# Rows of 450 words padded to 464, and the second cross attention in chunks of 512, 512, 512 and 66

## The chip, the core and the metric

The kernel runs on one core of a Trainium2 chip. The metric is the device time of one execution in microseconds (us). Before the change it is 2689.3 us, the median of three runs (2683.21 to 2691.54).

## What is computed

Two layers of a perceiver on 8 batches: 64 query tokens each, and a context of 1601 tokens, both 512 wide, in float32. Cut to what the change touches:

```python
x = x + xattn0(layernorm(x), ctx)   # 32 heads of 128, 8 key/value heads
x = x + mamba(layernorm(x))         # state-space scan over 64 steps
x = x + ternary_ffn(layernorm(x))
# second cross attention: one head, no weights
a = einsum('bqd,bkd->bqk', layernorm(x), ctx)
x = x + einsum('bqk,bkd->bqd', softmax(a), ctx)
x = x + self_attention(layernorm(x))
x = x + octonion_ffn(layernorm(x))
```

In the first cross attention, `k = ctx @ Wk + bk` and `v = ctx @ Wv + bv` are computed for all 1601 tokens, then `softmax(q k / sqrt(128)) v`. In the second, the scores are one 64 x 1601 table for each batch.

## The kernel before, in words

**The first cross attention** is most of the time (`x_all`). Its units are the 64 pairs of a batch and a key/value head. The context of a batch, transposed, stands in SBUF in four blocks of 384, 384, 384 and 450 tokens (`BLK`). `x_ctx` (line 295) brings each block in as four chunks of 128 channels: it loads a chunk into a staging tile `cst`, ScalarE copies it rounded (the "high" part, line 105), and GpSimd writes what is left over (the "low" part, line 106). The tile of a block is [128, 2, 4, width]: partition, high or low, chunk, token. The first three blocks lie in three buffers of the tile `cxb`, with rows of 384 words; the last block lies in the one buffer of `cxt`, with rows of 450 words. `cst` has rows of 450 words for all blocks. A product of two such operands is three matmuls: high by high, high by low, low by high.

- `x_v` (matmul at line 334) computes values for 128 tokens and two heads at a time: the block's tokens are the weights, `wv` with 256 columns is the moving operand. 12 matmuls for each token tile.
- `x_k` (line 363) computes a head's keys for one block: `wk` is the weights, the block with its 384 or 450 columns is the moving operand. 12 matmuls, then ScalarE and VectorE write the key tile `kt` (lines 108 and 109). `kt` is [128, 2, 450] whatever the block, three buffers.
- `x_s` (line 385) computes scores: a 128-token part of `kt` is the weights, `q` with 256 columns is moving. Three matmuls for each tile of tokens. Lines 388 and 392 take them out of PSUM and keep the maximum.
- `x_max`, `x_spread`, `x_exp`, `x_av`, `x_o` do the softmax and the product with the values for the unit before, between these steps. `x_wo` (line 511) is the output projection.

**The other layers** (`chain`) run for a group of two batches at a time, four groups. The first three run beside the first cross attention of later batches: `advance` lets a side chain go on as far as its planned cost (the numbers that the generators yield) says. Its work for VectorE, ScalarE and GpSimd is kept in program order (`Late`, `Side`); the rest of the order is set when the program is built, from a simulated time line (`schedule_with_timeline_sim=True`). The last group runs after the first cross attention, with other buffer counts (`tail`).

**The second cross attention** (`xattn1`, line 997) is one block of that chain. `scores` goes through the 1601 keys in parts of PSUM size: each entry of `GW` names the chunk of the score table and the widths of the loads. Each load brings `ctxT` columns for 4 chunks of 128 channels; four multiplications put two half sums into the upper and lower 64 partitions of PSUM (line 1021). ScalarE copies the lower half (line 1032), VectorE adds it to the upper half and writes a chunk of the table (line 1034). When all parts are there, VectorE takes a maximum by chunk (line 1040) and over the chunks (line 1041), and ScalarE computes the exponential by chunk with its sum (line 1044). `values` transposes the table in tiles of 128 keys (line 1059) and multiplies with `ctxN` (line 1077). Where a side chain runs, the same instructions are recorded at line 65, the helper that keeps them in order.

Before, the table has three chunks of 512, 512 and 577 (`SW`), the last one filled by two parts of 384 and 194 columns. In a side chain each chunk is a buffer of the tag `b2`, which has five buffers, each as large as the largest tile of the tag: the 578 words of the third chunk. In the last group the table is one tile `bc` of 1602 words.

Of the kernel before, what the change touches and what calls it, by code (L numbers as in the profile page):

```python
# [9 lines left out]
FR = mybir.dt.float32r  # L10
AF = mybir.ActivationFunctionType
ALU = mybir.AluOpType
AX = mybir.AxisListType
# [3 lines left out]
P = 128  # L17
D = 512
NC = 4
T = 64  # L20
# [4 lines left out]
NT = 13  # L25
TAIL = LK - 12 * P
BLK = [(0, 384), (384, 384), (768, 384), (1152, 450)]
LB = 3
DIN = 1024
NCH = 8  # L30
# [20 lines left out]
def rows_of(t):  # L51
    return TAIL if t == 12 else P
# [26 lines left out]
class Kernel:  # L79
# [133 lines left out]
    def q_ln(self, p):  # L213
# [9 lines left out]
        for g in range(ng):  # L223
            n = min(P, NQ - g * P)
            xs = self.sb("S", [P, 2, 256], pool=self.xp, bufs=SB)
            xt.append(xs[:n].rearrange("p a b -> p (a b)"))
# [68 lines left out]
    def x_ctx(self, b, k):  # L295

        nc = self.nc
        o, w = BLK[k]
        if k == LB:
            t = self.sb("cxt", [P, 2, NC, BLK[LB][1]], FR, pool=self.xp, bufs=1)  # L300
        else:
            t = self.sb("cxb", [P, 2, NC, BLK[0][1]], FR, pool=self.xp, bufs=3)
        for c in range(NC):
            st = self.sb("cst", [P, BLK[LB][1]], pool=self.xp, bufs=3)
            nc.sync.dma_start(out=st[:, :w], in_=self.i["ctxT"][b, c, :, o : o + w])
            self.split(t[:, 0, c, :], t[:, 1, c, :], st[:, :w], eng=nc.gpsimd)
        self.ctxb[(b, k)] = t
# [6 lines left out]
    def at(self, t):  # L314

        blk = min(t // 3, LB)
        return blk, (t - 3 * blk) * P
# [36 lines left out]
    def x_k(self, b, i, blk, w):  # L354

        nc = self.nc
        wd = BLK[blk][1]
        cx = self.cblk(b, blk)
        ps = self.px.tile([P, D], FP, name=self.nm("k_ps"), tag="kv", bufs=KVB)
        k = 0  # L360
        for c in range(NC):
            for a, m in ((0, 0), (0, 1), (1, 0)):
                nc.tensor.matmul(ps[:, :wd], lhsT=w[:, a, c, :], rhs=cx[:, m, c, :], start=k == 0, stop=k == 11)  # L363
                k += 1
        kt = self.sb("kt", [P, 2, BLK[LB][1]], FR, pool=self.xp, bufs=3)
        self.split(kt[:, 0, :wd], kt[:, 1, :wd], ps[:, :wd], bias=self.bk[:, i : i + 1])
        return kt

    def x_s(self, b, i, st):

        nc = self.nc
        q = self.q[(b, i)]
        S = self.S.setdefault((b, i), [])
        if st == 0:
            self.mf[(b, i)] = self.sb("mx", [P, 2, 256], pool=self.xp, bufs=1)
        mx = self.mf[(b, i)]
        for g in [(2 * st, 2 * st + 1)] + ([(12,)] if st == 5 else []):
            sp = self.px.tile([P, 2, 256], FP, name=self.nm("s_ps"), tag="kv", bufs=KVB)
            r = P
            for gi, t in enumerate(g):  # L380
# [3 lines left out]
                for k, (a, m) in enumerate(((0, 0), (0, 1), (1, 0))):  # L384
                    nc.tensor.matmul(sp[:r, gi, :], lhsT=kt[:, a, o : o + r], rhs=q[:, m, :], start=k == 0, stop=k == 2)  # L385
            s = self.sb("S", [P, 2, 256], pool=self.xp, bufs=SB)
            n = len(g)
            nc.scalar.copy(s[:r, :n], sp[:r, :n])  # L388
            if n == 1:
                nc.vector.tensor_tensor(mx[:r, 0], sp[:r, 0], mx[:r, 0], ALU.max)  # L390
            elif len(S) > 0:
                nc.vector.tensor_tensor(mx, sp, S[0] if len(S) == 1 else mx, ALU.max)  # L392
            S.append(s)
        if st == 5:
# [602 lines left out]
    def xattn1(self, bs, x, xo):  # L997

        nc, i = self.nc, self.i
        lt = self.lnT(x, P, hl=False)  # L1000
        GW = [(0, (256, 256)), (1, (256, 256)), (2, (192, 192)), (2, (194,))]
        SW = [512, 512, 577]
        TS = ((0, 4), (4, 8), (8, NT))

        def scores(k, b):
            q0 = k * T
            if self.tail:
                s = self.sb("bc", [T, LP])
                S = [s[:, :512], s[:, 512:1024], s[:, 1024:]]
            else:  # L1010
                S = [self.sb("b2", [T, 512]), self.sb("b2", [T, 512]), self.sb("b2", [T, 578])]
            o = 0
            for m, ws in GW:
                ps = self.acc()
                e = 0
                for w in ws:
                    cx = self.sb(self.tc4, [P, NC, 256])
                    nc.sync.dma_start(out=cx[:, :, :w], in_=i["ctxT"][b, :, :, o + e : o + e + w].rearrange("c p k -> p c k"))
                    for c in range(2):
                        for half in range(2):  # L1020
                            nc.tensor.matmul(  # L1021
                                ps[half * T : half * T + T, e : e + w],
                                lhsT=lt(2 * half + c, 0)[:, q0 : q0 + T],
                                rhs=cx[:, 2 * half + c, :w],
                                start=c == 0,
                                stop=c == 1,
                            )
                    e += w
                    if self.tail:
                        yield 2  # L1030
                lo = self.sb("b2", [T, D])
                nc.scalar.copy(lo[:, :e], ps[T:, :e])
                so = o - 512 * m
                nc.vector.tensor_tensor(S[m][:, so : so + e], ps[:T, :e], lo[:, :e], ALU.add)
                o += e
                if not self.tail:
                    yield 2 * len(ws)
            nm = self.sb("s1m", [T, 4])
            for m in range(3):
                nc.vector.tensor_reduce(nm[:, m : m + 1], S[m][:, : SW[m]], AX.X, ALU.max)  # L1040
            nc.vector.tensor_reduce(nm[:, 3:4], nm[:, 0:3], AX.X, ALU.max, negate=True)
            sm2 = self.sb("s1s", [T, 4])
            for m in range(3):
                nc.scalar.activation(S[m][:, : SW[m]], S[m][:, : SW[m]], AF.Exp, bias=nm[:, 3:4], accum_out=sm2[:, m : m + 1])
            sm = sm2[:, 3:4]
            nc.vector.tensor_reduce(sm, sm2[:, 0:3], AX.X, ALU.add)
            nc.vector.reciprocal(sm, sm)
            yield 3
            return S, sm

        def values(k, b, S, sm):
            q0 = k * T
            pts = []
            for m, (t0, t1) in enumerate(TS):
                pt = self.sb("b2", [P, 5, T])
                tp = self.acc().rearrange("p (t q) -> p t q", q=T)
                for t in range(t0, t1):
                    r = rows_of(t)
                    nc.tensor.transpose(tp[:r, t - t0, :], S[m][:, (t - t0) * P : (t - t0) * P + r], self.ident[:T, :T])
                e = min(t1, 12) - t0  # L1060
                nc.scalar.copy(pt[:, :e, :], tp[:, :e, :])
                if t1 == NT:
                    nc.scalar.copy(pt[:TAIL, e, :], tp[:TAIL, e, :])
                pts.append(pt)
                yield 2
            ps = self.acc()
            for t in range(0, NT, 2):
                two = t + 1 < NT
                r = rows_of(t)
                cx = self.sb(self.tc4, [P, 2, D])  # L1070
                if two:
                    nc.sync.dma_start(out=cx, in_=i["ctxN"][b, t * P : (t + 2) * P, :].rearrange("(u p) d -> p u d", p=P))
                else:
                    nc.sync.dma_start(out=cx[:r, 0], in_=i["ctxN"][b, t * P : t * P + r, :])
                m = min(t // 4, 2)
                for u in range(1 + two):
                    nc.tensor.matmul(  # L1077
                        ps[u * T : u * T + T], lhsT=pts[m][:r, t + u - TS[m][0], :], rhs=cx[:r, u], start=t == 0, stop=t + u >= NT - 2
                    )
                if self.tail:  # L1080
                    yield 1 + two
            if not self.tail:
# [407 lines left out]
```

## Time and profile before

| | |
|---|---|
| median of three runs | 2689.3 us |
| the profiled execution | 2687.19 us, of it the span of the profile 2685.1 us |
| mean granted TensorE clock | 0.983 |
| value projection, line 334 | 4992 matmuls, 1536 of them on `cxt` |
| key projection, line 363 | 3072 matmuls, 768 of them on `cxt` |
| scores, line 385 | 2496 matmuls, the weights from `kt` |
| second cross attention's scores, line 1021 | 448 matmuls in the trace (each multiplication is two) |
| loads of the last block, `cst` | 32 of 225 KB, 5.2 us to landing |

The profile names engines PE (TensorE matmul), PEld (its weight loads), DVE (VectorE), ACT (ScalarE), POOL (GpSimd) and SP (the queue that issues loads). A group line reads: line, engine, operation, output tile <- input tiles, shapes, count | busy us, mean ns of one | idle time of the engine just before these, and what ended it. Busy time counts overlapping instructions once, so for pipelined matmuls busy time by count is less than the mean of one. A line of the order of time reads: start, length of the merged run, engine, line, operation, tiles, shapes, count. The 40 digits are busy tenths in equal slices of the span, of 67 us each.

### The profile page before, as it was taken

What the parts mean: (1) busy time and instruction counts of PE and PEld (TensorE: products, weight loads), DVE (VectorE), ACT (ScalarE), POOL (GpSimd) and SP (SyncE); (2) the same over time, 40 slices, a digit from 0 to 9 for tenths busy, and PEclk for the clock granted to TensorE, in tenths of its full rate; (3) what the DMA queues carried; (4) which work ended last, traced back from release to release, by engine and by line L of the source; (5) the groups of instructions that cost most, each with busy time, mean ns of one, the idle gap of its engine ahead of it and who ended that gap; (6) DMA issues with size and microseconds to landing.
All of it is one profiled execution on the core that took longest, in us unless ns stands there. A gap on an engine that the chain in (4) does not pass through costs nothing.

```text
span 2685.1 us, 43976 instructions
## 1 busy us (share of the span) xinstructions
PE 2549.7 (95%) x16320; PEld 2269.3 (85%) x16320; DVE 1667.6 (62%) x2739; ACT 1350.2 (50%) x3128; POOL 1247.6 (46%) x1243
## 2 busy tenths in 40 slices
PE   7999999999999999999999999999999999977797
PEld 6988999999999899978989988988898898964544
DVE  4534357665687775545567676554657777668754
ACT  4545454344556554544555554544546545436433
POOL 2434463463368663521367457521239556405420
PEclk9999999999999999999999999999999999987899
DMA  9788876675213244764324452665343455466674
GB/s 308 225 295 276 281 239 190 203 240 180 67 66 105 68 133 150 232 190 145 97 98 148 149 161 89 216 201 164 102 135 92 137 159 155 143 226 216 234 261 166
DMA packets 311126, 466.08 MB, mean 174 GB/s; under 512 B 88440, under 2 KB 187768, under 8 KB 306432
## 3 DMA queue, kind: packets, MB, share of 16 engines
q1 hardware_dynamic: 310912, 463.28, 53.4%
q8 instruction: 128, 2.10, 0.3%
q14 instruction: 86, 0.70, 0.1%
HBM read 389.66 MB, written 73.53 MB: 173 GB/s over the span
## 4 chain that ended last, share of the span: by engine, by line
PE 68%; DMA 9%; DVE 9%; POOL 7%; issue 4%; ACT 3%; SPq 0%; POOLq 0%; DVEq 0%; ACTq 0%
PE v_ps L334 16%; PE k_ps L363 16%; PE o_ps L464 10%; PE s_ps L385 8%; POOL a L65 3%; PE w_ps L511 2%; PE acc L274 2%; DVE a L65 2%; PE acc L1077 2%; PE acc L801 2%; PE acc L1021 1%; PE acc L759 1%; PE acc L756 1%; POOL ss L452 1%; DMA b<-in_ctxT_dram 1%
## 5 line engine op out<-in xcount | busy, mean ns | idle before, releaser
L363 PE MATMUL k_ps<-cxb,wk 128*128 128x384 f32 x2304 | 470.3, 347 | 35.3 <-DVE mx L392 13.2
L334 PE MATMUL v_ps<-wv,cxb 128*128 128x256 f32 x3456 | 467.9, 281 | 1.0 <-DVE kt L109 0.6
L334 PEld LDWEIGHTS v_ps<-wv,cxb 128*128 128x128 f32 x3456 | 438.0, 188 | 19.3 <-issue 11.7
L363 PEld LDWEIGHTS k_ps<-cxb,wk 128*128 128x128 f32 x2304 | 405.3, 191 | 53.2 <-DVE mx L392 15.6
L464 PE MATMUL o_ps<-S,v 128*128 128x256 f32 (+1 forms) x1664 | 413.6, 381 | 7.4 <-DVE rw L479 4.0
L385 PE MATMUL s_ps<-q,kt 128*128 128x256 f32 (+1 forms) x2496 | 413.7, 299 | 5.2 <-DVE mx L392 2.4
L385 PEld LDWEIGHTS s_ps<-q,kt 128*128 128x128 f32 (+1 forms) x2496 | 342.8, 185 | 28.5 <-issue 6.9
L388 ACT COPY S<-s_ps 128x512 f32<-128x512 f32 (+1 forms) x448 | 241.9, 553 | 241.0 <-PE s_ps L385 236.6
L452 POOL TENSOR_TENSOR ss<-ss,S 128x512 f32<-128x512 f32 x254 | 349.3, 1375 | 14.7 <-ACT S L427 1.3
L392 DVE TENSOR_TENSOR mx<-s_ps,mx 128x512 f32<-128x512 f32 x256 | 175.1, 684 | 264.0 <-ACT S L388 262.7
L464 PEld LDWEIGHTS o_ps<-S,v 128*128 128x128 f32 (+1 forms) x1664 | 298.6, 190 | 46.7 <-issue 5.2
L429 POOL TENSOR_TENSOR ss<-S,S 128x512 f32<-128x512 f32 x64 | 84.5, 1320 | 469.4 <-ACT S L427 469.1
L108 ACT ACTIVATE kt<-k_ps,c_bk 128x384 fp32r<-128x384 f32 (+1 forms) x256 | 152.0, 594 | 246.9 <-PE k_ps L363 245.9
L426 DVE TENSOR_TENSOR S<-S,m_ps 128x512 f32<-128x512 f32 (+1 forms) x448 | 257.3, 640 | 20.5 <-PE m_ps L412 20.2
L427 ACT ACTIVATE S<-S 128x512 f32<-128x512 f32 (+1 forms) x448 | 246.7, 599 | 43.4 <-DVE S L426 42.7
L109 DVE SCALAR_TENSOR_TENSOR kt<-k_ps,c_bk,kt 128x384 fp32r<-128x384 f32 (+1 forms) x256 | 160.9, 629 | 158.0 <-ACT kt L108 156.5
L337 ACT COPY v<-v_ps 128x256 f32<-128x256 f32 (+1 forms) x416 | 152.5, 368 | 198.4 <-PE v_ps L334 196.0
L334 PE MATMUL v_ps<-wv,cxt 128*128 128x256 f32 (+1 forms) x1536 | 206.5, 282 | 1.5 <-DVE mx L392 1.0
L334 PEld LDWEIGHTS v_ps<-wv,cxt 128*128 128x128 f32 (+1 forms) x1536 | 192.7, 175 | 10.5 <-issue 3.4
L65 DVE TENSOR_TENSOR_SCAN a<-a,a 128x512 f32<-128x512 f32 x96 | 154.7, 1613 | 62.9 <-POOL a L65 62.8
L363 PE MATMUL k_ps<-cxt,wk 128*128 128x450 f32 x768 | 178.6, 375 | 1.4 <-DVE mx L392 1.3
L65 POOL TENSOR_TENSOR a<-a,bc 128x512 f32<-128x512 f32 x96 | 128.1, 1335 | 90.7 <-DVE a L65 90.7
(357 smaller groups left out, 3947.8 us busy)
## 6 DMA issues: line engine op xcount, KB each, us to landing
wo<-d_wo SPq DMA_DIRECT2D x128, 512.0 KB, 5.3
wk<-d_wk SPq DMA_DIRECT2D x63, 512.0 KB, 3.5
wv<-d_wv SPq DMA_DIRECT2D x31, 1024.0 KB, 5.7
cst<-in_ctxT_dram SPq DMA_DIRECT2D x96, 192.0 KB, 3.0
b<-in_ctxN_dram SPq DMA_DIRECT2D x36, 512.0 KB, 3.7
d_q<-q_t SPq DMA_DIRECT2D x32, 512.0 KB, 5.9
q<-d_q SPq DMA_DIRECT2D x64, 256.0 KB, 3.1
d_wo<-wo SPq DMA_DIRECT2D x32, 512.0 KB, 5.7
```

The lines of the kernel that those rows point to most:

```text
L65: return lambda *a, **k: self.tc.keep_in_program_order(f(*a, **k))
L109: eng.scalar_tensor_tensor(lo, src, bias, hi.bitcast(FP), ALU.add, ALU.subtract)
L334: nc.tensor.matmul(ps[:r], lhsT=cx[:, a, c, o : o + r], rhs=w[:, m, c, :], start=k == 0, stop=k == 11)
L337: nc.scalar.copy(vt[:r], ps[:r])
L363: nc.tensor.matmul(ps[:, :wd], lhsT=w[:, a, c, :], rhs=cx[:, m, c, :], start=k == 0, stop=k == 11)
L385: nc.tensor.matmul(sp[:r, gi, :], lhsT=kt[:, a, o : o + r], rhs=q[:, m, :], start=k == 0, stop=k == 2)
L388: nc.scalar.copy(s[:r, :n], sp[:r, :n])
L392: nc.vector.tensor_tensor(mx, sp, S[0] if len(S) == 1 else mx, ALU.max)
L426: nc.vector.tensor_tensor(sv, sv, ps[:r, 1:2].to_broadcast([r, w, 256]), ALU.add)
L427: nc.scalar.activation(sv, sv, AF.Exp, scale=ISC)
L452: nc.gpsimd.tensor_tensor(ss, ss, S[n], ALU.add)
L464: nc.tensor.matmul(ps[:, 0], lhsT=self.v[(b, j, t)][:r, hc : hc + P], rhs=S[t // 2][:r, t % 2], start=t == 0, stop=t == NT - 1)
```

## The change

A constant `ROW = 464` is added. The tiles `cxt` (its four channel chunks, high and low), `cst` and `kt` get rows of 464 words instead of 450; every access keeps its width, so the added words are never read or written. In the second cross attention the score table has four chunks of 512, 512, 512 and 66 (65 keys in the last), filled by four parts of the same sizes. The last chunk gets its own tile `s1x` with one buffer in a side chain, and a fourth slice of `bc` in the last group. The largest `b2` tile is then 512 words. There is one maximum and one exponential more for each batch, and the last tile of the transposes reads the fourth chunk.

```diff
+ROW = 464
...
-            t = self.sb("cxt", [P, 2, NC, BLK[LB][1]], FR, pool=self.xp, bufs=1)
+            t = self.sb("cxt", [P, 2, NC, ROW], FR, pool=self.xp, bufs=1)[:, :, :, :w]
...
-            st = self.sb("cst", [P, BLK[LB][1]], pool=self.xp, bufs=3)
+            st = self.sb("cst", [P, ROW], pool=self.xp, bufs=3)
...
-        kt = self.sb("kt", [P, 2, BLK[LB][1]], FR, pool=self.xp, bufs=3)
+        kt = self.sb("kt", [P, 2, ROW], FR, pool=self.xp, bufs=3)
...
-        GW = [(0, (256, 256)), (1, (256, 256)), (2, (192, 192)), (2, (194,))]
-        SW = [512, 512, 577]
+        GW = [(0, (256, 256)), (1, (256, 256)), (2, (256, 256)), (3, (66,))]
+        SW = [512, 512, 512, 65]
...
-                S = [s[:, :512], s[:, 512:1024], s[:, 1024:]]
+                S = [s[:, :512], s[:, 512:1024], s[:, 1024:1536], s[:, 1536:]]
             else:
-                S = [self.sb("b2", [T, 512]), self.sb("b2", [T, 512]), self.sb("b2", [T, 578])]
+                S = [*(self.sb("b2", [T, 512]) for _ in range(3)), self.sb("s1x", [T, 66], bufs=1)]
...
-            for m in range(3):
+            for m in range(4):
                 nc.vector.tensor_reduce(nm[:, m : m + 1], S[m][:, : SW[m]], AX.X, ALU.max)
-            nc.vector.tensor_reduce(nm[:, 3:4], nm[:, 0:3], AX.X, ALU.max, negate=True)
+            nc.vector.tensor_reduce(nm[:, 4:5], nm[:, 0:4], AX.X, ALU.max, negate=True)
...
-            for m in range(3):
-                nc.scalar.activation(S[m][:, : SW[m]], S[m][:, : SW[m]], AF.Exp, bias=nm[:, 3:4], accum_out=sm2[:, m : m + 1])
+            for m in range(4):
+                nc.scalar.activation(S[m][:, : SW[m]], S[m][:, : SW[m]], AF.Exp, bias=nm[:, 4:5], accum_out=sm2[:, m : m + 1])
...
-                    nc.tensor.transpose(tp[:r, t - t0, :], S[m][:, (t - t0) * P : (t - t0) * P + r], self.ident[:T, :T])
+                    src = S[m][:, (t - t0) * P : (t - t0) * P + r] if t < 12 else S[3][:, :r]
+                    nc.tensor.transpose(tp[:r, t - t0, :], src, self.ident[:T, :T])
```

More of the change, by code (lines that the diff above doesn't have):

```diff
@@ L1037, in scores @@
                     yield 2 * len(ws)
-            nm = self.sb("s1m", [T, 4])
-            for m in range(3):
+            nm = self.sb("s1m", [T, 5])
+            for m in range(4):
                 nc.vector.tensor_reduce(nm[:, m : m + 1], S[m][:, : SW[m]], AX.X, ALU.max)
-            nc.vector.tensor_reduce(nm[:, 3:4], nm[:, 0:3], AX.X, ALU.max, negate=True)
-            sm2 = self.sb("s1s", [T, 4])
-            for m in range(3):
-                nc.scalar.activation(S[m][:, : SW[m]], S[m][:, : SW[m]], AF.Exp, bias=nm[:, 3:4], accum_out=sm2[:, m : m + 1])
-            sm = sm2[:, 3:4]
-            nc.vector.tensor_reduce(sm, sm2[:, 0:3], AX.X, ALU.add)
+            nc.vector.tensor_reduce(nm[:, 4:5], nm[:, 0:4], AX.X, ALU.max, negate=True)
+            sm2 = self.sb("s1s", [T, 5])
+            for m in range(4):
+                nc.scalar.activation(S[m][:, : SW[m]], S[m][:, : SW[m]], AF.Exp, bias=nm[:, 4:5], accum_out=sm2[:, m : m + 1])
+            sm = sm2[:, 4:5]
+            nc.vector.tensor_reduce(sm, sm2[:, 0:4], AX.X, ALU.add)
             nc.vector.reciprocal(sm, sm)
```

## The prediction

> **What bounds the kernel now.** I read the busy shares and the 40 slices first, then a table of stretches, then the matmul groups, the order of time on the tensor engine, and last the rows of the second cross attention. The profiled execution took 2687.2 us (span 2685.1 and 2.1 around it); the median of the three runs is 2689.3, so 2.1 is added to a sum made on the profile.
>
> ```profile
> PE 2549.7 (95%) x16320; PEld 2269.3 (85%) x16320; DVE 1667.6 (62%) x2739; ACT 1350.2 (50%) x3128; POOL 1247.6 (46%) x1243
> PE   7999999999999999999999999999999999977797
> 500.00:1130.00 630.00, 620.52 (x4147) 590.36 (x4147) 422.65 (x667) 328.53 (x768) 346.06 (x352) 1.00 0.44 139
> 2430.00:2530.00 100.00, 73.48 (x419) 49.37 (x419) 90.59 (x135) 60.23 (x179) 63.45 (x64) 0.81 0.58 192
> ```
>
> The first two lines say that PE is the bound: 95% busy, and 9 in every slice but the first and four of the last five. The stretch rows (length, then busy PE, PEld, DVE, ACT, POOL, then clock, DMA share and GB/s) say where that holds. From 500 to 1130 us PE works 620.5 of 630 us; summed over the stretches from 60 to 2345 us it is 2233.5 of 2285, 98%. There a nanosecond saved on each of n matmuls is n ns of the end, and work on DVE, ACT or POOL is covered. After 2345 us PE works 272 of 341 us, and from 2430 to 2530 DVE is the fullest with 90.6 of 100.
>
> **Part 1, the padding.** It adds and removes no instruction. It moves the start of each row of 450 words, 1800 bytes, to 464 words, 1856 bytes. So I ask whether today's 450-word rows cost anything beside the 384-word rows of the other three blocks.
>
> ```profile
> L363 PE MATMUL k_ps<-cxb,wk 128*128 128x384 f32 x2304 | 470.3, 347 | 35.3 <-DVE mx L392 13.2 <-ACT cxb L105 10.4 <-DMA wk<-d_wk 9.2
> L363 PE MATMUL k_ps<-cxt,wk 128*128 128x450 f32 x768 | 178.6, 375 | 1.4 <-DVE mx L392 1.3 <-ACT v L337 0.2
> L109 DVE SCALAR_TENSOR_TENSOR kt<-k_ps,c_bk,kt 128x384 fp32r<-128x384 f32 x192 | 117.4, 612 | 98.5 <-ACT kt L108 97.3
> L109 DVE SCALAR_TENSOR_TENSOR kt<-k_ps,c_bk,kt 128x450 fp32r<-128x450 f32 x64 | 43.5, 679 | 59.6 <-ACT kt L108 59.2
> ```
>
> Reading rows as the moving operand (key projection, L363): busy time by matmul is 470.3/2304 = 204 ns for 384 columns, 0.53 a column, and 178.6/768 = 233 ns for 450, 0.52 a column. The 450-word rows pay nothing. Writing key tiles on DVE (L109): 679 - 612 = 67 ns for 66 columns, the same rate, and hidden besides. ACT's copy (580 and 635 ns) and POOL's split (1119 and 1172 ns, against 1315 for 512 columns) say the same.
>
> Reading rows as weights is different. The order of time shows runs of the value projection (L334), 12 matmuls of 256 columns each:
>
> ```profile
> 559.73 1.58 PE L334 MATMUL v_ps<-wv,cxb 128*128 128x256 f32 x12
> 563.58 2.89 PE L334 MATMUL v_ps<-wv,cxb 128*128 128x256 f32 x24
> ...
> 570.85 1.52 PE L334 MATMUL v_ps<-wv,cxb 128*128 128x256 f32 x12
> ...
> 585.25 2.99 PE L334 MATMUL v_ps<-wv,cxt 128*128 128x256 f32 x24
> ...
> 595.32 1.57 PE L334 MATMUL v_ps<-wv,cxt 128*128 128x256 f32 x12
> ```
>
> 24 less 12 is twelve more matmuls: on the aligned block (cxb) 2.89 - 1.52 = 1.37 us, 114 ns each; on the last block (cxt) 2.99 - 1.57 = 1.42 us, 118 ns each. So a matmul whose weights come from 450-word rows takes about 4.2 ns more, (2.99 - 2.89)/24. But the first line is a cxb run at the slow pace too: aligned rows allow the fast pace and don't secure it. Score matmuls (L385), whose weights are key tiles, also go slowly: a run of six takes 0.87 us, and less the last one's own 0.28 that is 0.59/5 = 118 ns.
>
> The bounds by matmul are 0 and 4.2 ns gained; a loss is excluded as far as these rows go, since the aligned block is never slower. Value projection on cxt: 1536 matmuls, 0 to 6.4 us. I take half, 3.2, because cxb runs show both paces. Scores: 2496 matmuls, 0 to 10 us. I take 1, because two of three of their weight loads read the first row of a key tile, which the padding doesn't move within the tile, and because each run restarts after a wait. Key projection: 0.
>
> The Trainium skill, "SBUF — State Buffer", section "Specifications (TRN2)", says that SBUF is read in 16-byte lines and that each crossing to a new line costs. 1800 bytes are 112.5 lines, so by it every second row begins in mid-line and all three readers should pay; the key projection's rows above show no such cost for the moving operand. By the rule the sum would be that of the first rival below.
>
> **Part 2, the chunks.** Line by line, for each of eight batches.
>
> ```profile
> L65 DVE TENSOR_REDUCE s1m<-b 64x1 f32<-64x512 f32 x12 | 7.9, 673 | 0.2
> L65 DVE TENSOR_REDUCE s1m<-b 64x1 f32<-64x577 f32 x6 | 4.4, 741 | 0.1
> ...
> L65 ACT ACTIVATE b<-b,s1m 64x512 f32<-64x512 f32 x12 | 8.6, 714 | 1.3 <-DVE s1m L65 1.3
> ...
> L65 ACT ACTIVATE b<-b,s1m 64x577 f32<-64x577 f32 x6 | 4.6, 765 | 0.0
> ```
>
> - PE: the same 28 multiplications over the same 1602 columns. By busy time 256 columns cost 27.1/192 = 141 ns and 192 cost 10.5/96 = 109, so 0.5 a column and 46 for 66. A batch had 32 x 141 + 16 x 109 + 8 x 110 = 7.1 us and gets 48 x 141 + 8 x 46 = 7.1 us. Zero.
> - DVE: (741 - 673)/65 = 1.05 ns a column, so the new reduce of 65 costs 673 - 447 x 1.05 = 205 ns, and the third becomes 68 shorter: +0.14 us. The additions that empty PSUM (679, 546 and 346 ns for 512, 384 and 194) are linear: 512 and 66 cost what 384 and 194 did.
> - ACT: 0.78 ns a column, so the exponential of 65 costs 714 - 447 x 0.78 = 364 ns, less 51 on the third: +0.31 us. The accumulator's reading (188 ns) comes once more, which may add its length: 0.31 to 0.50.
> - Latency: behind the last chunk's matmuls stood a copy of 318, an addition of 346 and a reduce of 741 ns; now about 211, 213 and 205. The maximum is ready 0.78 us sooner, the sum of exponentials 0.31 to 0.50 us later in work.
> - DMA: seven loads as before; in KB 4 x 512, 2 x 384 and 388 become 6 x 512 and 132. The total is equal.
>
> In the main stretch PE's 98% hides DVE and ACT: six batches cost nothing, and 6 x 0.45 = 2.7 us if the cover were gone. Two of the eight batches run beside the last group's scan from 2380 to 2530 us, where DVE is the fullest, and two in the last group itself from 2546 us. There 4 x 0.14 on DVE and 4 x 0.31 on ACT, 1.8 us, stand against 4 x 0.78 = 3.1 us of latency; from 2546 to 2590 the chain of waits is nearly all PE, so little of either shows. Bounds +1.8 and -3.1; I take +0.5, as the DVE stretch is the nearer row.
>
> The Trainium skill, "DMA: Bandwidth & Descriptors", section "Specifications", speaks against this part: below 512 bytes a transfer isn't at line rate, and 66 columns are rows of 264 bytes. No row here has that size. Priced as rows of 512 bytes (an estimate from that page) the last load would count as 256 KB, still less than the 388 it replaces.
>
> **The sum.** 2687.2 - 3.2 - 1.0 + 0.5 = 2683.5 by the profile, 2685.6 beside the median. About 0.3%, 8.1 us, is what a measurement of this kernel can tell from no change, so this counts as the same.
>
> **Rivals.**
> 1. The rows' start is what holds all these matmuls at 118 ns. Then 6.4 from the values, up to 10 from the scores and some 1.5 from the key projection: 10 to 18 us, about 2675. For it: no cxt run in those lines is at the fast pace. Against it: cxb runs at 1.58 us, and the score runs' waits.
> 2. Slower. The third chunk now waits for two loads of 512 KB where it waited for 384 KB. The issue rows have 4.6 us to landing for one and 3.3 for the other, so its matmuls can be due 2 x 1.3 = 2.6 us later, and PE takes its instructions in the order written, so the main stream queues behind them. The last load is smaller (the nearest row, 170 KB, lands in 2.3 us instead of 4.6), but nothing gets that back if the stream has already stood. Six side batches: 15.6 us; from four of them on, 10.4 us, it decides. For it: waits of PE's L1021 for in_ctxT total 7.8 us in 5 places. Against it: all but 0.2 of these lie after 2345 us, so before that the loads are early. The builder also orders the free instructions by simulated times, so a few such waits can appear elsewhere (PE's k_ps waited 14.4 us for DVE's mx, 9 times). About 2700.
> 3. The padding does nothing: 118 ns comes from the order of the work, not the rows' start. 2687.2 + 0.5 + 2.1 = 2689.8.
>
> **How the numbers follow.** Forecast 0.28, rival 1 0.25, rival 2 0.27, rival 3 0.20. The forecast and rival 3 lie within 0.3%: same 0.48, faster 0.25, slower 0.27. The range leaves out a tenth on each side: from 2689.3 less the 18 us of rival 1, near 2671, to 2703, near rival 2's full price of 15.6.
>
> **What would show it.** Right: runs of 24 on cxt at 2.89 to 2.99 us, some of them fast; L1021's busy time unchanged at some 59 us for all eight batches; a fourth reduce near 205 ns and a fourth exponential near 364. Rival 1: every cxt run at 1.52 and score runs of six below 0.87 us. Rival 2: new PE waits of L1021 for in_ctxT before 2345 us. Rival 3: cxt at 118 ns as now. It would be wrong altogether if a write or read by another engine changed its rate with the new row starts, or if the padding moved the last group's buffers onto ones that are released later.

## The result, and the profile after

| | before | after |
|---|---|---|
| median | 2688.4 us (2683.21 to 2691.54) | 2707.3 us (2703.78 to 2710.1) |
| ratio after / before | | 1.007, 95% interval 1.0058 to 1.0082 |
| the profiled execution | 2687.19, span 2685.1 | 2703.78, span 2702.0 |
| mean granted clock | 0.983 | 0.979 |

The change makes the kernel slower by 18.9 us, 0.7%. Predicted were 2685.6 us, and the time lies above the predicted range (2671 to 2703). The two profiled executions differ by 16.9 us of span, and that is what their traces have to explain. Busy times and starts come from one execution of each kernel, while executions of the kernel before alone lie up to 16 us apart (2676.88 to 2692.93 in 29 of them), so the ratios below rest on all executions and not on the traces.

The page of the changed kernel, the rows that answer to those of before (the busy shares, the tenths of PE, the two stretches):

```profile
PE 2559.1 (95%) x16320; PEld 2278.4 (84%) x16320; DVE 1671.7 (62%) x2747; ACT 1352.5 (50%) x3144; POOL 1244.9 (46%) x1243
PE   7999999999999999999999998999999999976787
500.00:1130.00 630.00, 619.86 (x4130) 590.05 (x4129) 422.97 (x662) 326.46 (x762) 348.72 (x355) 1.00 0.44 137
2430.00:2530.00 100.00, 71.35 (x431) 50.01 (x429) 87.84 (x133) 62.46 (x190) 62.96 (x63) 0.80 0.57 187
```

The main stretch is as full as before (619.9 of 630 us, before 620.5). Beside one 8 in the middle, what differs is the last four digits, 6787 in place of 7797, which points at the end. The groups and the order of time that answer to part 1:

```profile
L335 PE MATMUL v_ps<-wv,cxb 128*128 128x256 f32 x3456 | 474.7, 282 | 1.9 <-DVE mx L393 1.3 <-DVE kt L110 0.6
L364 PE MATMUL k_ps<-cxb,wk 128*128 128x384 f32 x2304 | 469.0, 345 | 34.9 <-DVE mx L393 11.7 <-ACT cxb L106 11.1 <-DMA wk<-d_wk 7.3
L364 PE MATMUL k_ps<-cxt,wk 128*128 128x450 f32 x768 | 179.7, 375 | 1.2 <-DVE mx L393 1.2
L110 DVE SCALAR_TENSOR_TENSOR kt<-k_ps,c_bk,kt 128x384 fp32r<-128x384 f32 x192 | 117.3, 611 | 102.6 <-ACT kt L109 101.7
L110 DVE SCALAR_TENSOR_TENSOR kt<-k_ps,c_bk,kt 128x450 fp32r<-128x450 f32 x64 | 43.6, 681 | 49.3 <-ACT kt L109 48.9
```

```profile
501.21 2.99 PE L335 MATMUL v_ps<-wv,cxb 128*128 128x256 f32 x24
508.58 1.57 PE L335 MATMUL v_ps<-wv,cxb 128*128 128x256 f32 x12
...
523.07 2.97 PE L335 MATMUL v_ps<-wv,cxt 128*128 128x256 f32 x24
532.75 1.58 PE L335 MATMUL v_ps<-wv,cxt 128*128 128x256 f32 x12
```

Key projection and key tiles are unchanged. The value projection did the opposite of what was hoped: runs on the padded block are as slow as before (2.97 and 1.58 us), and the runs on the first three blocks, a mix of 1.52 and 1.58 us before, are now nearly all slow. Their 3456 matmuls take 474.7 us, before 467.9.

**Where the 16.9 us arise.** A group's self-attention and its octonion feed-forward each begin with a layernorm, so the instructions that write `ln_st` mark where a group stands. After 2590 us there are three: the last group's before its self-attention, the third group's before its octonion feed-forward, the last group's before its feed-forward. The order of time on DVE, before:

```profile
2593.39 0.68 DVE L141 BATCH_NORM_STATS2 ln_st<-xr 128x6 f32<-128x512 f32 x1
2595.82 0.69 DVE L141 BATCH_NORM_STATS2 ln_st<-xr 128x6 f32<-128x512 f32 x1
2646.45 0.69 DVE L141 BATCH_NORM_STATS2 ln_st<-xr 128x6 f32<-128x512 f32 x1
```

and after:

```profile
2594.99 0.68 DVE L142 BATCH_NORM_STATS2 ln_st<-xr 128x6 f32<-128x512 f32 x1
2632.14 0.68 DVE L142 BATCH_NORM_STATS2 ln_st<-xr 128x6 f32<-128x512 f32 x1
2647.72 0.68 DVE L142 BATCH_NORM_STATS2 ln_st<-xr 128x6 f32<-128x512 f32 x1
```

The last group stands where it stood (1.6 and 1.3 us later). The third group is 36 us later. The same holds of the order itself: counted in the traces, 81 vector instructions stood from the third group's marker to the end, now 61. From the last marker to the end it was 2685.1 - 2646.45 = 38.7 us and is 2702.0 - 2647.72 = 54.3: of the 16.9 us, 15.6 fall here, beside the last group's feed-forward. The matmul groups from 2648 us on say what else runs there. The third group's feed-forward matmuls read weights from the tile `w_r`; before:

```profile
L759 PE MATMUL acc<-w_r,b_r 128*128 128x512 f32 x7 | 3.0, 423 | 0.6 <-DVE b_r L106 0.5
L756 PE MATMUL acc<-w_r,b_r 128*128 128x512 f32 x6 | 2.5, 412 | 1.1 <-ACT b_r L105 1.1
```

and after:

```profile
L757 PE MATMUL acc<-w_r,b_r 128*128 128x512 f32 x19 | 9.3, 489 | 0.6 <-ACT b_r L106 0.6
L760 PE MATMUL acc<-w_r,b_r 128*128 128x512 f32 x19 | 8.8, 462 | 0.0
```

With their 336-column rows (8 + 8 in both), 29 of these matmuls lay behind 2648 us, now 54. The rows of the four groups overlap; counted once, these matmuls kept PE busy for 7.0 us there, now for 15.1. PE's whole busy time after that point rises from 26.8 to 37.6 us. So work that stood among the last group's self-attention now stands among its feed-forward. It also decides the end. The last feed-forward matmuls of the third group (`w_r`) and of the last group (`w`), before:

```profile
2667.64 0.39 PE L759 MATMUL acc<-w_r,b_r 128*128 128x512 f32 x1
2680.93 0.40 PE L759 MATMUL acc<-w,b 128*128 128x512 f32 x1
```

and after:

```profile
2687.37 0.39 PE L760 MATMUL acc<-w,b 128*128 128x512 f32 x1
2697.56 0.63 PE L760 MATMUL acc<-w_r,b_r 128*128 128x512 f32 x1
```

Before, the last group ended last; now its matmuls end 6 us later and the third group's come 10 us after them. No instruction there was changed by the diff. The trace says where the time went; why the third group came late had to be tried.

### The profile page after: what moved, and what is told of

Read it like the earlier page. It is cut to its first block, busy times and chain, and to the rows that moved or that the text cites. A ratio compares the mean times of both kernels' runs of the same rounds, so it can differ in the third digit from the quotient of the medians.

```text
span 2702.0 us, 44015 instructions
## 1 busy us (share of the span) xinstructions
PE 2559.1 (95%) x16320; PEld 2278.4 (84%) x16320; DVE 1671.7 (62%) x2747; ACT 1352.5 (50%) x3144; POOL 1244.9 (46%) x1243
## 4 chain that ended last, share of the span: by engine, by line
PE 73%; DVE 8%; POOL 7%; DMA 6%; issue 3%; ACT 3%; SPq 0%; POOLq 0%; DVEq 0%; ACTq 0%
PE v_ps L335 17%; PE k_ps L364 16%; PE o_ps L465 10%; PE s_ps L386 8%; POOL a L66 3%; PE w_ps L512 3%; PE acc L275 2%; DVE a L66 2%; PE acc L802 2%; PE acc L1079 2%; PE acc L757 2%; PE acc L760 2%; POOL ss L453 1%; PE acc L1022 1%; PE m_ps L413 1%
## 5 line engine op out<-in xcount | busy, mean ns | idle before, releaser
L335 PE MATMUL v_ps<-wv,cxb 128*128 128x256 f32 x3456 | 474.7, 282 | 1.9 <-DVE mx L393 1.3
L335 PEld LDWEIGHTS v_ps<-wv,cxb 128*128 128x128 f32 x3456 | 444.6, 188 | 19.9 <-issue 11.4
L335 PE MATMUL v_ps<-wv,cxt 128*128 128x256 f32 (+1 forms) x1536 | 205.4, 283 | 4.1 <-DVE kt L110 3.2
L66 DVE TENSOR_TENSOR_SCAN a<-a,a 128x512 f32<-128x512 f32 x96 | 160.9, 1676 | 61.0 <-POOL a L66 60.9
L66 ACT ACTIVATE a<-lv,c_A_log 128x128 f32<-128x128 f32 x384 | 122.6, 392 | 96.8 <-DVE a L66 96.5
```

The costliest lines, as they stand in the source:

```text
L66: return lambda *a, **k: self.tc.keep_in_program_order(f(*a, **k))
L335: nc.tensor.matmul(ps[:r], lhsT=cx[:, a, c, o : o + r], rhs=w[:, m, c, :], start=k == 0, stop=k == 11)
```

## The experiments

The expectations of the first four kernels name three theories: **A** gives a part of the loss to the chunks and a part to the padding, by way of the slower value projection; **B** gives all to the chunks, **C** all to the padding.

**e1** has the new chunks with rows of 450.

```diff
-ROW = 464
+ROW = 450
```

> The new chunks with the rows left at 450 words. Every engine has the instructions of the changed kernel in the same order; only addresses in SBUF differ, and those of the first cross attention are the ones of before. Theory A (two causes: where wv lies sets the pace of the value projection, about 5 us by 1130 us; the new order of the last 340 us costs the other 12): value runs at the mix of before (busy time of L334 on cxb 468 us, not 475), start of the mamba scan's stage 4 us earlier than in the changed kernel, about 2702 us. Theory B (all of it comes from the chunks): 2707 us. Theory C (all of it comes from the padding): 2688 us.

Measured: 2705.95 us, ratio 1.0071 (1.0048 to 1.0094). The value projection is back at 468.8 us, and the time is that of the whole change. C falls. B's 2707 us is nearer than A's 2702, but the interval, some 6 us to either side, holds both.

**e2** is e1 with an unused tile of 384 bytes ahead of `wv`, so that `wv` lies where the padding puts it, at byte 104000 of a partition in place of 103616.

```diff
+            self.gap = self.sb("gap", [P, 96], pool=self.xp, bufs=1)
+            nc.gpsimd.memset(self.gap[:, :1], 0.0)
```

> As e1_chunks_only, rows of 450 words, but with an unused tile of 384 bytes ahead of wv, so that wv and what lies behind it have the addresses of the changed kernel (and one memset of one column more at the start). Theory A (the address of wv sets the pace): as the changed kernel, 2707 us, value runs on cxb at 118 ns, L334 busy 475 us. Rival (the padded rows themselves are read more slowly): as e1_chunks_only, value runs at the mix of before, L334 468 us.

Measured: 2707.56 us, 1.0072 (1.0054 to 1.0091); the value projection takes 474.1 us. So its pace follows the address of `wv`, not the length of any row. In the total the 5 us don't show beside e1.

**e3** has the new chunks and pads `cxt` alone, which leaves `wv` at its old address.

```diff
-ROW = 464
+ROW = 450
+ROWT = 464
...
-            t = self.sb("cxt", [P, 2, NC, ROW], FR, pool=self.xp, bufs=1)[:, :, :, :w]
+            t = self.sb("cxt", [P, 2, NC, ROWT], FR, pool=self.xp, bufs=1)[:, :, :, :w]
```

> The new chunks with only cxt padded to 464 words; wv and kt keep the addresses of before. Theory A: as e1_chunks_only in every stage before 2345 us, runs on cxt at 118 ns though their rows are aligned. Rival (450-word rows hold these matmuls at 118 ns, as the prediction's first part had it): runs on cxt at 114 ns in part, 3 to 6 us less busy time on L334. Rival (padded rows are slower): cxt runs above 118 ns.

Measured (one execution): 2704.75 us; the first three blocks 468.7 us, the padded block's matmuls still at 118 ns. Rows that begin at multiples of 16 bytes bring nothing to the operand for which they were made.

**e4** is the change, but the last group keeps 512, 512 and 577: only the side chains have the new chunks.

```diff
...
+        GW = [(0, (256, 256)), (1, (256, 256)), (2, (192, 192)), (2, (194,))] if self.tail else [(0, (256, 256)), (1, (256, 256)), (2, (256, 256)), (3, (66,))]
+        SW = [512, 512, 577] if self.tail else [512, 512, 512, 65]
...
```

> The padding as in the changed kernel, the new chunks in the first three groups only; the last group's second cross attention keeps chunks of 512, 512 and 577. Theory A says that the last 340 us lose 12 us by the order in which the last two groups' work is interleaved. If that order is upset by the last group's own chunks, this is near 2695 us; if by the third group's, which end beside it, near 2707 us. A rival (the last group's extra maximum and exponential cost the time) gives at most 2 us less than the changed kernel, 2705 us.

Measured: 2709.45 us, 1.0077 (1.0058 to 1.0097). The chunks of the side chains are enough, though their own work is covered by PE's full main stretch. That leaves two ways for them to act on the end: **theory O**, the order in which the builder puts the last two groups' instructions, and **theory W**, the work and the waits of the new instructions. The next four tell them apart.

**e5** is the whole change with one planner constant altered, which touches the last group's chain alone. Every engine's order is that of the changed kernel up to matmul 13523 of 14334; in the traces PE's orders part at 2403 us.

```diff
-SPAN = [3.1,3.1,2.6,0.2]
+SPAN = [3.1,3.1,2.6,0.4]
```

> The changed kernel whole (padding and new chunks in all groups), with one planner constant of the last stage altered: the last group's span in the plan 0.4 instead of 0.2. Every engine's order stays that of the changed kernel until the last two groups' chains (matmul 13523 of 14334); there the third group's feed-forward is put where the kernel before has it. Theory O (the loss is where the builder puts the third group's last steps among the last group's): the third group's feed-forward layernorm is back at about 2597 us instead of 2632, and the time is that of before plus the 4 us that the main stream was late: 2688 to 2696. Theory W (the loss is the work of the chunks themselves: one maximum and one exponential more in each round, matmuls of 66 columns): nothing of that is taken away, so 2705 to 2709.

Measured: 2686.94 us, ratio to before 1.0004 (0.9992 to 1.0016), 1 us below what theory O gave. With all of the change's work in it, the loss is gone. The markers of its trace:

```profile
2588.41 0.69 DVE L142 BATCH_NORM_STATS2 ln_st<-xr 128x6 f32<-128x512 f32 x1
2589.73 0.69 DVE L142 BATCH_NORM_STATS2 ln_st<-xr 128x6 f32<-128x512 f32 x1
2639.45 0.69 DVE L142 BATCH_NORM_STATS2 ln_st<-xr 128x6 f32<-128x512 f32 x1
```

The third group is back beside the last group's self-attention, and only 6 of its feed-forward matmuls, 1.9 us of PE, are left after 2648 us. (The profiled execution took 2679.62 us, 7.3 below the median; the ratio, not its span, is the measure.)

**e6**, the control, is the kernel before with the same constant.

> The control of e5: the kernel before with the same constant 0.4 in the place of 0.2. Its order on the engines is as before up to the last two groups' chains, and differs little there. Both theories: as before within 4 us, 2686 to 2694; if it gains or loses as much as e5 does, e5 says nothing of the chunks.

Measured: 2691.47 us, 1.0016 (1.0004 to 1.0027): nothing gained, rather 4 us lost. So 0.4 is not a better setting in itself.

**e7** has rows of 450 and the new chunks in the last group alone.

```diff
-ROW = 464
+ROW = 450
...
+        SW = [512, 512, 512, 65] if self.tail else [512, 512, 577]
...
```

> Old row lengths; the new chunks in the last group alone, where nothing else stands beside them but the third group's end; the first three groups keep 512, 512 and 577. The order of the engines is that of the kernel before up to the last stage, and the third group's feed-forward layernorm keeps its place. Theory O: as before, 2688 to 2692. Theory W with the last group as its place (the chain of the last group is what ends last): 2700 to 2707.

Measured: 2690.72 us, 1.0013 (1.0003 to 1.0024). Where nothing covers them, the new chunks cost 3.5 us (0.8 to 6.4 by the interval). The third group is 10 us later than before in this trace, but 8 of these are there when the first cross attention ends (2393.1 us, before 2384.8), so they don't come from the last group's chunks.

**e8** is the kernel before with the third group's span shortened in the plan: no instruction added, another order.

```diff
-SPAN = [3.1,3.1,2.6,0.2]
+SPAN = [3.1,3.1,2.4,0.2]
```

> The kernel before, with the third group's span in the plan 2.4 instead of 2.6: no instruction added or taken away, but the third group's feed-forward layernorm stands 59 instead of 79 vector instructions from the end, near the 60 of the changed kernel (the order of side blocks differs from about 2000 us on too). Theory O: slower than before without one new chunk, 2698 to 2710. Theory W: as before, 2686 to 2693, since it has none of the added work.

Measured: 2727.19 us, 1.0145 (1.0119 to 1.0171). The old work in a bad order loses twice what the change lost, above what theory O gave, because here all the third group's feed-forward, 70 matmuls and 21.8 us of PE, falls behind 2648 us. In the traces PE's order differs from 1902 us on, so it isn't the change's loss again, only the same mechanism.

**o1 and o2** ask which part of the chunks upsets the order. o1 takes the widths alone, with three chunks and not one instruction added; o2 the split maximum and exponential alone, with the old loads.

```diff
-        GW = [(0, (256, 256)), (1, (256, 256)), (2, (192, 192)), (2, (194,))]
+        GW = [(0, (256, 256)), (1, (256, 256)), (2, (256, 256)), (2, (66,))]
```

```diff
...
+            nc.vector.tensor_reduce(nm[:, 3:4], S[2][:, 512:577], AX.X, ALU.max)
...
+            nc.scalar.activation(S[2][:, 512:577], S[2][:, 512:577], AF.Exp, bias=nm[:, 4:5], accum_out=sm2[:, 3:4])
...
```

> Rows of 450 and three chunks of 512, 512 and 577 as before, but the third chunk is filled by parts of 512 and 66 columns in place of 384 and 194: the widths of the loads and matmuls of the change, without its fourth maximum and exponential. The number of instructions is that of before on every engine. In the order as built, the third group's feed-forward layernorm stands 71 vector instructions from the end (79 before, 60 in the changed kernel). Theory O: slower than before though nothing is added, by the 8 of 19 steps that it is moved or more: 2696 to 2710. Theory W: no work is added and the table is ready up to 0.6 us sooner for each batch, 2684 to 2691. Rival 2 of the prediction (the third chunk's two loads of 512 KB come later): waits of the score matmuls for the context, 2 us and more in each batch.

> Rows, loads and parts as before; only the maximum and the exponential of the third chunk are split into 512 and 65 columns, one vector and one scalar instruction more for each batch. In the order as built, the third group's feed-forward layernorm stands 71 vector instructions from the end, as in o1. Theory O: as o1, 2696 to 2710. Theory W: 0.2 us on the vector engine and 0.4 on the scalar engine for each batch, at most 8 x 0.6 = 4.8 us if nothing hid it, half of it in the batches of the tail: 2689 to 2694.

Measured: o1 2703.76 us, 1.0065 (1.0045 to 1.0084); o2 2712.03 us, 1.009 (1.0075 to 1.0105). Each alone loses about as much as both together; o2 lies 2 us above what theory O gave. o1 is the plainest case: its first cross attention ends at 2384.9 us, before at 2384.8, its score matmuls wait for the context 6.1 us in all (before 7.8), and its markers are

```profile
2598.14 0.68 DVE L141 BATCH_NORM_STATS2 ln_st<-xr 128x6 f32<-128x512 f32 x1
2633.59 0.69 DVE L141 BATCH_NORM_STATS2 ln_st<-xr 128x6 f32<-128x512 f32 x1
2659.10 0.69 DVE L141 BATCH_NORM_STATS2 ln_st<-xr 128x6 f32<-128x512 f32 x1
```

The third group is 38 us later with nothing added anywhere. W falls. All kernels that have a ratio on one scale (markers in us; "late work" is PE's busy time on the third group's feed-forward after 2648 us; "behind it" counts, in the trace, the vector instructions from the third group's marker to the end, one to three more than in the order as built, of which the expectations speak):

| | third group | last group | late work | behind it | ratio to before |
|---|---|---|---|---|---|
| e10 | 2593.8 | 2645.0 | 5.5 | 82 | 0.9959 |
| e9 | 2596.7 | 2647.6 | 7.0 | 82 | 0.9988 |
| before | 2595.8 | 2646.5 | 7.0 | 81 | 1 |
| e5 | 2589.7 | 2639.5 | 1.9 | 82 | 1.0004 |
| e7 | 2605.4 | 2649.5 | 8.5 | 78 | 1.0013 |
| e6 | 2606.4 | 2655.5 | 11.2 | 81 | 1.0016 |
| o1 | 2633.6 | 2659.1 | 18.8 | 73 | 1.0065 |
| after | 2632.1 | 2647.7 | 15.1 | 61 | 1.007 |
| e1 | 2634.7 | 2650.3 | 15.3 | 61 | 1.0071 |
| e2 | 2636.9 | 2652.5 | 16.3 | 61 | 1.0072 |
| e4 | 2627.1 | 2664.1 | 15.0 | 73 | 1.0077 |
| o2 | 2640.2 | 2666.6 | 19.5 | 73 | 1.009 |
| e8 | 2647.9 | 2670.3 | 21.8 | 62 | 1.0145 |

Below 2607 us for the third group the time is that of before within 0.2% (but for e10's gain); from 2627 on, 0.65% and more are lost. (e6's profiled execution lies 8 us above its median, so its markers are late for the ratio beside them.) The count "behind it" parts the same kernels, 78 and more from 73 and less. In the lower part of the table the third group's last matmul is the last of the kernel; e4 is the exception, where the last group still ends last and is itself 18 us later than before.

**m1 and m2: what sets 113 or 118 ns.** The padding's term stood apart from all this, so the disputed matmul was measured by itself. m1 leaves the whole computation out and runs the value projection's pattern on one large tile at chosen addresses, 24 matmuls for each pair.

```diff
...
+    [(50432, 384, OLD + 32 * k) for k in range(17)]
...
+    + [(s + 512 * o, 384, m) for m in (OLD, NEW) for s in (50432, 62720, 75008) for o in range(3)]
...
```

> Leaves the whole computation out and measures the value projection's matmuls by themselves: groups of 12 of 128x128 by 128x256 in fp32r with the kernel's pattern of rows, 55 pairs of addresses of the weight rows and the streamed rows (the old and the new place of the V weights, steps of 32 bytes between them, steps of 1 KB beyond; the context blocks' three slots and the last block's with rows of 450 and 464 words) with no other engine at work, and then 8 pairs beside vector, scalar and GpSimd instructions on other tiles. Theory of the address by itself: 113 ns a matmul at 103616 and 118 at 104000, in the quiet part too, with a step at some address between. Theory of contention (the address only sets which other engine's tile is close by): one pace in the whole quiet part, and a slower one in the busy part or none. Theory of row alignment: 118 for rows of 450 words as stationary operand and 113 for rows of 464.

Measured, 216 matmuls each (nine pairs of 24, no other engine at work): the first stretch has `wv`'s old address against the three slots of `cxb`, the second its new one.

```profile
125.40:149.80 24.40, 24.40 (x217) 24.40 (x217) 0.00 (x0) 0.00 (x0) 0.00 (x0) 1.00 0.00 1
149.90:175.20 25.30, 25.30 (x217) 25.30 (x216) 0.00 (x0) 0.00 (x0) 0.00 (x0) 1.00 0.01 1
```

24.4 us by 216 is 113 ns, 25.3 is 117. Start to start, the median is 113 at 103616 and 118 at 104000, with and without other engines at work (113.3 and 117.8 on average in the busy part). In steps of 32 bytes, one of eight is fast, every 256 bytes; beyond, all steps of 1 KB are fast. (VectorE and loads were still filling the tile beside most of the 32-byte steps, until 95.6 us; the nine pairs had neither.) The last block's pairs have a median of 118 (117.5 to 118.5) with rows of 450 and of 464 words. That the address by itself can set the pace is shown. Contention and row alignment as what tells 113 from 118 here: wrong. But the pair isn't all that counts in the kernel: all nine pairs at the old address run at 113 alone, while in the kernel before only some six of ten of their matmuls start 112 to 114 ns after the one ahead of them in a run, and most of the others 115 to 119. What slows those there no run shows.

**m2** moves the two operands apart and together, in the same manner.

> Leaves the whole computation out, as m1 did, and measures pairs of addresses of fp32r matmuls with no other engine at work. m1 gave 113.3 ns where the streamed rows begin 192 bytes past a multiple of 256 and the weight rows at a multiple of 256, and 117 to 120 at the seven other steps of 32 bytes, with all rows multiples of 256 bytes long. Theory of the pair (the difference of the two starts modulo 256 decides): when the weight rows move by 32 to 224 bytes the pace falls to 117 to 120, when both move together it stays 113; the last block with rows of 512 words runs at 113 at one step of eight and at 118 at the others, so that padding to 464 words, whose rows begin at four different steps, could not help. Theory of the streamed operand (its own start decides): the shift of the weight rows alone changes nothing, and the last block runs at 113 with rows of any length. For the key projection (128 by 384 and 128 by 450 columns) and the scores (sums of 3) both expect one pace about 3 to 5 ns under the others at some step, or none at all.

Measured: moving the weight rows alone by 32 to 224 bytes gives 117.9 to 120.1 ns, moving both by 32 gives 113; but moving both by 96 gives 117.7. Four bytes to either side of the fast place give 119 and 121. So the pair decides and not either start, though the difference of the two starts alone doesn't explain the 117.7. (VectorE and loads were still filling the tile during the shifts by 32 bytes and more, until about 90 us; the rows of 512 words, below, ran with neither.) With rows of 512 words the last block runs at 113 at one of eight steps and at 118 to 120 at the others. The key projection varies from 173.3 to 176.8 ns for 384 columns and from 200.6 to 207.3 for 450, the scores from 117.2 to 120.1. The theory of the streamed operand falls. What in the chip makes it so stays open.

**e9** is e5 with rows of 450: the same order, the old address of `wv`.

> As e5 (last group's span 0.4 in the plan, new chunks in all groups) with the rows back at 450, so that the block of the V weights lies at its old address, 384 bytes lower; every engine's order is the same as in e5 up to the last chains. What it tells is the worth of the padding at a settled order. Theory of the address (the value projection's matmuls of the first three blocks run at a mix of 113 and 118 ns with the old address, at 118 with the new): 467 to 469 us for the 3456 matmuls in place of 474.9, and, since they lie on the chain that sets the end, 3 to 7 us less than e5: ratio to before 0.998 to 0.9995. Theory of no worth (the faster matmuls only wait longer): ratio within 0.001 of that of e5, 1.0004. The theory that the prediction had (rows that begin on 16-byte lines spare 0 to 6 us): slower than e5 by up to 6 us.

Measured: 2683.97 us, 0.9988 (0.9977 to 0.9998); value projection on the first three blocks 468.3 us, in e5 474.9. Against e5 the padding costs 0.0016 of the time, some 4 us, with an uncertainty as large (0.0012 and 0.00105 combined, 0.0016), so that neither of the first two theories is excluded.

**e10** is e9 with the last block's rows 512 words apart, from 134400 on, the pair that m2 had found fast.

```diff
-            t = self.sb("cxt", [P, 2, NC, ROW], FR, pool=self.xp, bufs=1)[:, :, :, :w]
+            t = self.sb("cxt", [P, 16 + 2 * NC * 512], FR, pool=self.xp, bufs=1)
+            t = t[:, 16:].rearrange("p (m c w) -> p m c w", m=2, c=NC)[:, :, :, :w]
```

> e9 (new chunks, last group's span 0.4 in the plan, 450 words in the staging and key tiles) with the last context block's rows 512 words apart and its start 64 bytes later, at 134400, so that every row of it begins at a multiple of 256 bytes, as the first three blocks' rows do; 450 words of each row are used as before. All engines' orders are those of e9. Theory of the pair of addresses (m2 measured 113 ns for just this pair of tiles, 118 for rows of 450 and 464): the 1536 value projection matmuls of the last block fall from 118 towards 113 ns, at most 7 us of busy time and about half of it in the total, ratio to before 0.996 to 0.998. Theory that the last block's matmuls are held at 118 by what stands beside them in the kernel: no change from e9, 0.9988.

Measured: 2680.78 us, 0.9959 (0.9944 to 0.9973): faster than before by 0.4%, the best of all. Its order of time on the padded block:

```profile
587.13 2.99 PE L336 MATMUL v_ps<-wv,cxt 128*128 128x256 f32 x24
597.60 1.53 PE L336 MATMUL v_ps<-wv,cxt 128*128 128x256 f32 x12
```

Here the third token tile runs at the fast pace (1.53 us; 1.58 in e5 and in the changed kernel), the first two still at the slow one, though m2 had this pair at 113; the 1536 matmuls fall from 204.6 us in e9 to 203.6. That is 1 us where up to 7 were hoped for, and the ratios of e9 and e10 differ by 0.0029 (with an uncertainty of 0.0018), 8 us. The profiled execution of e10 took 2685.44 us, 4.7 above the median, so its trace can't show the rest. That e10 is faster than before is measured; where most of its gain over e9 comes from is open.

## Why the prediction was wrong

**What bounds the kernel**: right. PE's main stretch behaves as said, and added work on DVE and ACT is hidden in it.

**Part 1, the padding, -3.2 and -1.0**: wrong in its reason. The two paces seen in the trace were real, but I put the difference down to row starts because the one block that never ran fast was also the one with odd rows; from the slow runs of the other blocks I took only that aligned rows don't secure the fast pace, not that rows may have nothing to do with it. e3 and m1 show 118 ns with aligned rows. The busy time of the padded block fell from 206.5 to 205.4 us, by 1.1 where I took 3.2 (6.4 at most), the scores' rose by 1.3 us where I took a gain of 1, and what I had not priced at all, that padded tiles move the tiles behind them, made 3456 other matmuls 6.8 us slower. In the total that is about 4 us (e5 against e9), no more than its uncertainty. The Trainium skill, "SBUF — State Buffer", section "Specifications (TRN2)", speaks of 16-byte lines: in m1 all steps of 32 bytes begin on such a line, and one is at 113 ns, the other seven at 117 to 120. Lines are not what tells these apart.

**Part 2, the chunks**: the lengths of the instructions were right. The reduce of 65 takes 202 ns (205 said), the exponential 336 (364 said), and L1022's busy time is 55.3 us where L1021 had 57.7 (59 said). The loads of short rows cost nothing that shows: 132 KB landed in 3.1 us in the side chains and 6.0 in the last group, where the 388 KB that they replace took 4.6 and 7.3. e7 puts the chunks of the last group at 3.5 us, more than the 0.9 of two batches by my prices (2 x 0.45), which the interval, 0.8 to 6.4, just holds. **The step that failed is the term +0.5**, with its bounds of +1.8 and -3.1, and the sentence "from 2546 to 2590 the chain of waits is nearly all PE, so little of either shows". It counted what the instructions take where they stand, and took for granted that everything else keeps its place. In place of +0.5 the new order of the last two groups costs nearly all of the 18.9 us: with another order and the same work e5 is at 1.0004. Order had been named once, in rival 2 ("the builder also orders the free instructions by simulated times, so a few such waits can appear elsewhere"), but as a source of a few waits. It is a term of its own: o1, with nothing added, loses 0.65%, about 17 us, and o2, with 0.6 us of work for each batch, 24 us. I stopped the chain of waits at 2590, and the loss lies after 2630.

**Rivals.** Rival 2 came nearest by its number, 2700, and was wrong in its mechanism: waits of these matmuls for the context fell from 7.8 to 2.1 us, and a 512 KB load of the side chains landed in 3.9 us, before in 4.6. Rival 1 fell with the row starts. Rival 3 was right that the padding has no use, but gave the order of the work as the reason for 118 ns, where m1 shows the addresses, and missed the end.

**What would show it.** One sign of being wrong did come, in a place where it costs nothing: GpSimd changed its rate with the rows of `cxt` (see the last section). I had read its mean of 1172 ns as one pace with the other widths; it was a mix of two.

## What to carry to other kernels

Where the order of instructions is decided when the kernel is built, from estimated times, an edit can have a second cost: price the edit, and then ask what stands at the end and how late it may come. The tail is where it showed here, where PE works 272 of 341 us and so covers less; a marker for each chain (here the layernorms) tells in three lines which chain was moved. Before an edit is called bad, build it with the schedule's own constants moved a little: here the same work took 2687 or 2707 us.

## What the runs showed of the hardware

A 128x128 by 128x256 fp32r matmul in a steady stream, each with its own weight load, took 113 ns or 117 to 120 ns (119 and 121 four bytes off) by the addresses of its two operands alone, at a granted clock of 1.00. With no other engine at work this is shown for the nine pairs at the two places of `wv` (m1) and for the eight steps of rows of 512 words (m2); it is 4 to 6% that no row of a profile names. The Trainium skill, "TensorE: Matmul & The Clock Gate", section "Back-to-back issue gap", gives N / 2.4 + 2.5 ns for an isolated matmul, which is 109 ns for 256 columns (an estimate from that formula), and says that the weight load sets the spacing too; of addresses that section says nothing. No stream of m1 or m2 reached 109.

GpSimd's split of the last block (128x450) also follows the length of the rows of `cxt`. With rows of 450 words its least time is 971 to 981 ns in all nine kernels that have them, and it is every second chunk of channels that is fast (before: 1167, 981, 1156, 1287, 1133, 983 ns for the first six); with rows of 464 or 512 words the least is 1122 to 1147 ns in all five. e3, which pads `cxt` alone, is among these (1138), so neither the staging tile nor the keys do it. The middle value hides it: 1154 ns before, 1156 after. So the padding made every second split some 17% slower. In the total it doesn't show: e3, with `cxt` padded, took 2704.75 us, and e1, with rows of 450, 2705.95. Why the shorter rows are faster wasn't tried.
